# Three graph-attention layers and a gated graph network: first group's attention scores formed on TensorE, layer-norm scale applied in the normalization, new planner durations

## The chip, the cores and the metric

The kernel runs on one core of one Trainium2 chip. Its time is the device time in microseconds of one execution; every figure given as "the time" is the median of several executions. The profile is one execution recorded by the hardware profiler. Each engine of the core (TensorE or PE for matrix products, VectorE or DVE, ScalarE or ACT, GpSimd or POOL, SyncE or SP for transfers) runs its own list of instructions in order; the engines meet at semaphores.

## The reference

There are 128 graphs of 128 nodes with 256 features, all in 32-bit floats. Three attention layers and one recurrent layer follow each other, each on a layer-normalized input and with the input added back:

```python
for l in range(3):                                     # layers 0 to 2
    h  = maximum(layernorm(x), 0)                      # (x - mean) / sqrt(var + eps)
    Wh = h @ W[l]
    e  = (Wh @ a1)[:, :, None] + (Wh @ a2)[:, None, :] # one score for each pair of nodes
    e  = where(e > 0, e, 0.2 * e)
    p  = softmax(where(adj > 0, e, -9e15), axis=-1)
    x  = x + elu(p @ Wh)                               # layer 2: times the node mask first
h = maximum(layernorm(x), 0)
s = h
for i in range(3):                                     # layer 3: gated graph network
    m = A.T @ (s @ weight[i])                          # A = (adj != 0)
    s = gru_cell(m, s)                                 # gates r, z and candidate n
x = x + s
```

## The kernel before, in words

**Tiling.** The 128 graphs are cut into 33 groups (`SIZES`, `FIRST`): the first and the last have two graphs, the others four. A group goes through the three attention layers (`gat`, which calls `attention` once per layer) and then through three recurrent steps (`gru`). In `attention`, node number is the partition and the features lie along the free dimension. In `gru`, features are on the partitions and a group's nodes (512, or 256 in the small groups) are the columns of the products.

**Order.** Nothing is emitted in the order of the source. Every instruction is handed to a planner (`Plan.add`) with its engine, a cost in us, a rank (its due time) and the tiles it reads and writes. `Plan.issue` then runs a list scheduler: on each engine it takes, of the instructions that could start within 0.1 us of the earliest, the one of lowest rank, and moves simulated time on by the cost. Fixed lags stand for semaphores (PE 0.26, DVE and ACT 0.2, POOL 0.15). The order that it finds is the program. So a cost that is changed anywhere can change the order everywhere, though no instruction is added. The costs are small functions: `pe(cols)` at L260, `dve(cols)`, `act(cols)`. The ranks put attention of group 0 at -9, -7 and -5, of group 1 at -6.5, -4.5 and -2.5, and the preparation of the recurrent weights (`SETUP`) at -4; a recurrent step i of group g has rank 3g + i.

**Preparation.** `attention_weights` computes, per layer, the two vectors W·a1 and W·a2 on VectorE (L304, tile `wa`), which stand feature by feature on the partitions; TensorE transposes them and ScalarE copies them (L316) into `va`, where every partition holds both vectors whole. The recurrent weights are products of `gweight` and `w_ih` (L380, tile `wcp`, copied by L387). All of them come before any recurrent step of groups 0 and 1 (`last_setup`).

**Attention, groups 0 and 1** (`far` is false for g < 2). `stats` takes mean and variance (L423, L425), the negative mean `nm` (L430), and on GpSimd variance plus epsilon (L432) and its power of -0.5, `rs` (L434). ScalarE forms `xn` = relu(x - mean) (L507) *without* the scale. A score is one VectorE instruction, `scr` (L515): `xn` times the scalar `rs` of the node times a vector of `va`, summed over the features into `e`; there are two per graph. TensorE turns the second score into a row (L546); VectorE adds the two scores and masks them by a minimum with `cap` (L557, once per graph). Then leaky ReLU (L569), maximum (L571), exponential on ScalarE (L575), reciprocal and product with it (L582 to L586), a transpose on TensorE (L599, `atp`), and a VectorE product of the transposed weights with `rs` (L606, `at`), which puts the scale back. `ahp` (L627) is the product of the attention weights with `xn`, copied to `ah` by ScalarE (L634), `hp` (L646) the product with W; L660 to L664 form elu and the sum in `xo`.

**Attention, groups from 2 on** (`far`). The scale is applied in the normalization: `nm` is multiplied by `rs` (L503) and the activation has `rs` as its scale; the score has the constant 1.0 in place of `rs`. Row and transpose go by way of DRAM (`er`, `at`) instead of TensorE.

**Recurrent steps.** `agp` (L813) aggregates over the graph, copied to `ag` (L821); `nn`, `r`, `z`, `ni` (L790) are the gate products, twelve per half of 128 features; L843 to L880 are the gates on ScalarE and VectorE.

**Buffers.** PSUM has the tags `gat` (2 banks), `gru` (5) and `tr` (1); the pool `gw` has two buffers per tag, `ah` among them.

The cost of the narrow products and the two places where the scale enters before:

```python
    def pe(cols):
        return 0.035 + cols / 600 if cols <= P else 0.01 + cols / 600
...
                scale=rs.t[:, b : b + 1] if far else 1.0,
...
                scr.t, xn.t[:, b, :], 1.0 if far else rs.t[:, b : b + 1], VA[l].t[:, s, :],
...
                rs.t.rearrange("p (g o) -> p g o", o=1).to_broadcast([P, n, N]), op=OP.mult,
```

Of the kernel before, what the change touches and what calls it, by code (L numbers as in the profile page):

```python
# [185 lines left out]
def kernel(  # L186
# [27 lines left out]
    KD = D // P  # L214
    G = 4
    FAR = 2
    SIZES = [2] + [G] * ((B - 4) // G) + [2]
    NG = len(SIZES)
    FIRST = [sum(SIZES[:g]) for g in range(NG)]
# [20 lines left out]
    def const_val(name, shape):  # L240
        return plan.val(const, name, 1, lambda: const.tile([P, *shape], FT, name=name))

    def val(pool, tag, shape, name, bufs=2, dtype=FT, cut=None):

        def make():
            if pool is None and not rw_pool:
                setup.close()
                rw_pool.append(ctx.enter_context(tc.tile_pool(name="rw", bufs=2)))
            p = rw_pool[0] if pool is None else pool
            t = p.tile([P, *shape], dtype, tag=tag, name=name, bufs=bufs)  # L250
            return t if cut is None else t[:, :cut]
        return plan.val(pool, tag, bufs, make)

    def bank(tag, name):
        n = BANKS[tag]
        return plan.val(
            psum, tag, n, lambda: psum.tile([P, T], FT, tag=tag, name=name, bufs=n)
        )

    def pe(cols):  # L260
        return 0.035 + cols / 600 if cols <= P else 0.01 + cols / 600

    def dve(cols):
        return 0.12 + cols / 1000
# [16 lines left out]

    W, VA = [], []

    def attention_weights(l, w, a):
        rank = 1.5 * l - 8.0
        wt, va = const_val(f"w_{l}", [KD, D]), const_val(f"va_{l}", [2, D])
        first = l - 11.2
        load(256, first, lambda: nc.sync.dma_start(  # L290
            wt.t, w.rearrange("(k p) o -> p k o", p=P)), writes=[wt])
        ar = val(su, "ar", [2 * D], f"ar_{l}")
        load(2, first - 0.1, lambda: nc.sync.dma_start(
            ar.t[:1, :], a.rearrange("n o -> o n")), writes=[ar])

        ab = bank("gat", f"ab_{l}")
        add("PE", pe(T), rank, lambda: nc.tensor.matmul(
            ab.t, ones[:1, :], ar.t[:1, :], start=True, stop=True), reads=[ar], writes=[ab])
        wa = val(su, "wa", [2, KD], f"wa_{l}")
        vp = bank("gat", f"vp_{l}")  # L300

        def one(s, k):
            scr = val(su, "scr", [D], f"scr_{l}_{k}_{s}")
            add("DVE", dve(D) + 0.08, rank, lambda: nc.vector.scalar_tensor_tensor(  # L304
                scr.t, wt.t[:, k, :], 1.0, ab.t[:, s * D : (s + 1) * D], op0=OP.mult, op1=OP.mult,
                accum_out=wa.t[:, s, k : k + 1],
            ), reads=[wt, ab], writes=[scr, (wa, (s, k))])
            c = s * KD + k
            add("PE", 0.11, rank, lambda: nc.tensor.transpose(
                vp.t[:, c * P : (c + 1) * P], wa.t[:, s, k : k + 1].to_broadcast([P, P]), ident  # L310
            ), reads=[(wa, (s, k))], writes=[(vp, c)])

        for s in range(2):
            for k in range(KD):
                one(s, k)
        add("ACT", act(T), rank, lambda: nc.scalar.copy(  # L316
            va.t.rearrange("p s d -> p (s d)"), vp.t), reads=[vp], writes=[va])
        W.append(wt)
        VA.append(va)

    for l, (w, a) in enumerate(((w0, a0), (w1, a1), (w2, a2))):
        attention_weights(l, w, a)
# [91 lines left out]
    def stats(xt, n, name, rank, takes):  # L414

        st = val(gw, "st", [G, 6], f"st_{name}", cut=n)
        mv = val(gw, "mv", [G, 2], f"mv_{name}", cut=n)
        nm = val(gw, "nm", [G], f"nm_{name}", cut=n)
        ve = val(gw, "ve", [G], f"ve_{name}", cut=n)
        rs = val(gw, "rs", [G], f"rs_{name}", bufs=3, cut=n)  # L420

        def one(b):
            add("DVE", dve(D), rank, lambda: nc.vector.bn_stats(st.t[:, b, :], xt.t[:, b, :]),  # L423
                reads=[(xt, b)], writes=[(st, b)], takes=[mv, nm, ve, rs, *takes])
            add("DVE", 0.13, rank, lambda: nc.vector.bn_aggr(mv.t[:, b, :], st.t[:, b, :]),  # L425
                reads=[(st, b)], writes=[(mv, b)])

        for b in range(n):
            one(b)
        add("DVE", 0.16, rank, lambda: nc.vector.tensor_scalar(  # L430
            nm.t, mv.t[:, :, 0], -1.0, None, op0=OP.mult), reads=[mv], writes=[nm])
        add("POOL", 0.3, rank, lambda: nc.gpsimd.tensor_scalar(  # L432
            ve.t, mv.t[:, :, 1], EPS, None, op0=OP.add), reads=[mv], writes=[ve])
        add("POOL", 1.04, rank, lambda: nc.gpsimd.tensor_tensor(  # L434
            rs.t, ve.t, mhalf[:, :n], op=OP.pow), reads=[ve], writes=[rs])
        return nm, rs
# [54 lines left out]
    def attention(g, l, xt, cap, xo):  # L491
# [2 lines left out]
        rank = 3.0 * g - lead(g) + 2.0 * l  # L494
        xn = val(gw, "xn", [G, D], f"xn_{name}", cut=n)
        e = val(gw, "e", [2, G], f"e_{name}")
        far = g >= FAR
        nm, rs = stats(xt, n, name, rank, [xn, e, xo, cap])

        if far:
            add("DVE", 0.16, rank, lambda: nc.vector.tensor_mul(nm.t, nm.t, rs.t),  # L503
                reads=[nm, rs], writes=[nm])

        def centred(b):
            add("ACT", 0.45, rank, lambda: nc.scalar.activation(  # L507
                xn.t[:, b, :], xt.t[:, b, :], AF.Relu, bias=nm.t[:, b : b + 1],
                scale=rs.t[:, b : b + 1] if far else 1.0,
            ), reads=[(xt, b), nm, *([rs] if far else [])], writes=[(xn, b)])  # L510


        def score(b, s):
            scr = val(gw, "scr", [D], f"scr_{name}_{b}_{s}")
            add("DVE", dve(D), rank, lambda: nc.vector.scalar_tensor_tensor(  # L515
                scr.t, xn.t[:, b, :], 1.0 if far else rs.t[:, b : b + 1], VA[l].t[:, s, :],
                op0=OP.mult, op1=OP.mult, accum_out=e.t[:, s, b : b + 1],
            ), reads=[(xn, b), rs, VA[l]], writes=[scr, (e, (s, b))])

        for b in range(n):  # L520
            centred(b)
        for b in range(n):
            score(b, 1)
            score(b, 0)

# [3 lines left out]


        em = val(gw, "em", [G, N], f"em_{name}", cut=n)
        if far:
            de = plan.val(
                dram, f"de{n}", 2, lambda: dram.tile([P, n], FT, tag=f"de{n}", name=f"de_{name}")
            )
            er = val(gw, "er", [N * G], f"er_{name}")
            load(2, rank, lambda: nc.sync.dma_start(de.t, e.t[:, 1, :n]),
                reads=[(e, (1, b)) for b in range(n)], writes=[de], takes=[er, em])
            load(64 * n, rank, lambda: nc.sync.dma_start(
                er.t[:, : N * n], de.t.rearrange("p n -> (p n)").partition_broadcast(P)  # L540
            ), more=1.6, reads=[de], writes=[er])
        else:
            e2 = bank("gat", f"e2_{name}")
# [15 lines left out]
                cap.t[:, b, :], op0=OP.add, op1=OP.min,  # L559
            ), reads=[er if far else (e2, b), (e, (0, b)), cap], writes=[(em, b)])  # L560

        for b in range(0 if far else n):
            row(b)
        for b in range(n):
            masked(b)
        nmx = val(gw, "nmx", [G], f"nmx_{name}", cut=n)
        sm = val(gw, "sm", [G], f"sm_{name}", cut=n)
        ri = val(gw, "ri", [G], f"ri_{name}", cut=n)
# [3 lines left out]
            nmx.t, em.t, axis=AX.X, op=OP.max, negate=True), reads=[em], writes=[nmx])  # L572

        def power(b):
            add("ACT", 0.42, rank, lambda: nc.scalar.activation(  # L575
                em.t[:, b, :], em.t[:, b, :], AF.Exp, bias=nmx.t[:, b : b + 1],
                accum_out=sm.t[:, b : b + 1],
            ), reads=[(em, b), nmx], writes=[(em, b), (sm, b)])
# [4 lines left out]
        if l == 2:  # L583
            add("DVE", 0.16, rank, lambda: nc.vector.tensor_mul(
                ri.t, ri.t, nmT.t[:, FIRST[g] : FIRST[g] + n]), reads=[ri, nmT], writes=[ri])
        add("DVE", dve(n * P), rank, lambda: nc.vector.tensor_tensor(  # L586
            em.t, em.t, ri.t.rearrange("p (g o) -> p g o", o=1).to_broadcast([P, n, N]), op=OP.mult
        ), reads=[em, ri], writes=[em])

# [13 lines left out]
        if not far:  # L603
            for b in range(n):
                turn(b)
            add("DVE", dve(n * P), rank, lambda: nc.vector.tensor_tensor(  # L606
                at.t, atp.t[:, : n * P].rearrange("p (g i) -> p g i", g=n),
                rs.t.rearrange("p (g o) -> p g o", o=1).to_broadcast([P, n, N]), op=OP.mult,
            ), reads=[atp, rs], writes=[at])

        def turned_weights(b):
            if far:
# [57 lines left out]
    def gat(g):  # L670
# [27 lines left out]
            reads=[nm, rs], writes=[nm])  # L698

        def normed(b):  # L700
            add("ACT", 0.45, rank, lambda: nc.scalar.activation(
                hn.t[:, b, :], xt.t[:, b, :], AF.Relu, bias=nm.t[:, b : b + 1],
                scale=rs.t[:, b : b + 1],
            ), reads=[(xt, b), nm, rs], writes=[(hn, b)])
# [264 lines left out]
```

## Time and profile before

| what | value |
|---|---|
| median of 3 executions | 2757.75 us (2756.5 to 2758.16) |
| the profiled execution | 2757.73 us, span 2756.0 us |
| TensorE busy | 2712.8 us, 98% of the span |
| VectorE busy | 2082.3 us, 76% |
| ScalarE busy | 1280.4 us, 46% |
| GpSimd busy | 293.7 us, 11% |
| matrix instructions | 9563 |

The span runs from the first to the last instruction; the execution's own time is 1.7 us longer. "Busy" is the union of an engine's recorded instructions. In the profile's name for a group of instructions, `out<-in` gives the tiles, `x` the count, and the number behind the engine the source line. A 32-bit product is recorded as two matrix instructions (passes), so a product of 128 columns counts as x2. Transposes are single instructions. "Idle before, releaser" is the time for which the engine waited just before the group, and what ended the wait.

### The profile page before, as it was taken

Reading aid. Unit: us, or ns where it says so; the run is one execution under the profiler, and the core shown is the slowest. Engines: PE = TensorE matmul, PEld = TensorE weight load, DVE = VectorE, ACT = ScalarE, POOL = GpSimd, SP = SyncE. Lnnn points to the kernel's source line nnn. Section 1 sums busy time; section 2 is a strip of 40 time slices with the busy share of each in tenths; the row PEclk is TensorE's granted clock in tenths of the full one; section 3 lists DMA queues with packets and bytes.
Section 4 is the critical chain, followed back from the end, with each engine's and each line's share of the span. In section 5 each row is a group of like instructions: output and inputs, shape, how many; then the busy total and the mean of one; then the engine's idle time right before and its main releaser. Section 6 shows DMA issues by size and latency. Waiting matters only on the chain.

```text
span 2756.0 us, 32248 instructions
## 1 busy us (share of the span) xinstructions
PE 2712.8 (98%) x9563; PEld 1569.7 (57%) x9563; DVE 2082.3 (76%) x5541; ACT 1280.4 (46%) x2709; POOL 293.7 (11%) x369
## 2 busy tenths in 40 slices
PE   7899999999999999999999999999999999999998
PEld 4755555555555555555555555555555555555546
DVE  7778888778768887877788687778768886876643
ACT  4545444444444454444454445444444444444433
POOL 1111110101101101110111111111101010100000
PEclk9999999999999999999999999999999999999999
DMA  3113334433324433333333344323334333333310
GB/s 91 51 58 100 88 95 101 111 94 86 97 80 108 108 99 78 101 91 96 105 97 83 87 105 104 109 75 91 97 88 110 103 93 86 94 74 93 79 44 12
DMA packets 503094, 245.30 MB, mean 89 GB/s; under 512 B 280580, under 2 KB 472068, under 8 KB 502919
## 3 DMA queue, kind: packets, MB, share of 16 engines
q1 hardware_dynamic: 502918, 243.25, 33.5%
q8 instruction: 76, 1.25, 0.2%
q14 instruction: 100, 0.81, 0.1%
HBM read 139.28 MB, written 103.87 MB: 88 GB/s over the span
## 4 chain that ended last, share of the span: by engine, by line
PE 88%; DVE 8%; ACT 2%; DMA 1%; issue 1%; POOL 0%; SPq 0%; DVEq 0%; ACTq 0%; POOLq 0%
PE z L790 21%; PE r L790 21%; PE hp L646 11%; PE ni L790 11%; PE nn L790 10%; PE ahp L627 6%; PE agp L813 5%; DVE em L557 1%; DVE scr L515 1%; DVE xo L662 1%; DVE xo L664 1%; DVE d L877 1%; ACT em L575 1%; DVE h L880 1%; DVE n L856 0%
## 5 line engine op out<-in xcount | busy, mean ns | idle before, releaser
L790 PE MATMUL nn<-h,whh 128*128 128x512 f32 (+1 forms) x792 | 395.6, 581 | 1.9 <-DVE h L880 1.9
L790 PE MATMUL r<-ag,wc 128*128 128x512 f32 (+1 forms) x792 | 395.2, 581 | 1.3 <-ACT ag L821 1.3
L790 PE MATMUL ni<-ag,wc 128*128 128x512 f32 (+1 forms) x792 | 394.4, 579 | 1.4 <-ACT ag L821 1.4
L790 PE MATMUL z<-ag,wc 128*128 128x512 f32 (+1 forms) x792 | 394.2, 579 | 0.0
L790 PE MATMUL z<-h,whh 128*128 128x512 f32 (+1 forms) x792 | 394.2, 579 | 0.0
L790 PE MATMUL r<-h,whh 128*128 128x512 f32 (+1 forms) x792 | 394.2, 579 | 0.0
L851 DVE SCALAR_TENSOR_TENSOR n<-r,wn 128x512 f32<-128x512 f32 (+1 forms) x198 | 132.6, 670 | 336.5 <-ACT r L848 336.0
L646 PE MATMUL hp<-w,ah 128*128 128x256 f32 x1536 | 373.2, 381 | 0.5 <-ACT ah L634 0.2
L646 PEld LDWEIGHTS hp<-w,ah 128*128 128x128 f32 x1536 | 290.1, 190 | 131.4 <-issue 95.7
L515 DVE SCALAR_TENSOR_TENSOR scr<-xn,va 128x256 f32<-128x256 f32 x732 | 266.4, 423 | 33.9 <-ACT xn L507 33.6
L848 ACT ACTIVATE r<-r,brz 128x512 f32<-128x512 f32 (+1 forms) x198 | 133.2, 673 | 284.3 <-PE r L790 282.0
L813 PEld LDWEIGHTS agp<-am,hn 128*128 128x128 f32 x1536 | 202.3, 191 | 85.7 <-issue 73.5
L790 PEld LDWEIGHTS ni<-ag,wc 128*128 128x128 f32 x792 | 149.8, 190 | 177.9 <-issue 171.0
L790 PEld LDWEIGHTS r<-h,whh 128*128 128x128 f32 x792 | 149.3, 190 | 169.4 <-issue 162.8
L790 PEld LDWEIGHTS z<-h,whh 128*128 128x128 f32 x792 | 148.7, 190 | 168.3 <-issue 158.3
L821 ACT COPY ag<-agp 128x512 f32<-128x512 f32 (+1 forms) x198 | 113.0, 571 | 263.2 <-PE agp L813 262.8
L790 PEld LDWEIGHTS z<-ag,wc 128*128 128x128 f32 x792 | 148.4, 190 | 142.4 <-issue 138.2
L575 ACT ACTIVATE em<-em,nmx 128x128 f32<-128x128 f32 x384 | 149.4, 391 | 168.2 <-DVE nmx L571 166.4
L790 PEld LDWEIGHTS r<-ag,wc 128*128 128x128 f32 x792 | 146.1, 190 | 135.4 <-issue 120.5
L627 PEld LDWEIGHTS ahp<-at,xn 128*128 128x128 f32 x1536 | 191.3, 195 | 49.4 <-issue 37.6
L813 PE MATMUL agp<-am,hn 128*128 128x128 f32 x1536 | 205.3, 275 | 6.4 <-ACT hn L802 3.9
L526 POOL TENSOR_SCALAR xo<-xo 128x1024 f32<-128x1024 f32 (+1 forms) x66 | 73.2, 1110 | 1215.6 <-DVE xo L664 989.8
(94 smaller groups left out, 3474.1 us busy)
## 6 DMA issues: line engine op xcount, KB each, us to landing
d_hn<-tr_hn SPq DMA_DIRECT2D x116, 256.0 KB, 2.4
hn<-d_hn SPq DMA_DIRECT2D x464, 64.0 KB, 2.3
er<-de SPq DMA_DIRECT2D x90, 256.0 KB, 3.9
d_at<-tr_at SPq DMA_DIRECT2D x90, 256.0 KB, 2.0
at<-d_at SPq DMA_DIRECT2D x360, 64.0 KB, 2.0
x<-in_x_dram SPq DMA_DIRECT2D x31, 512.0 KB, 4.4
d_h<-tr_h SPq DMA_DIRECT2D x31, 512.0 KB, 2.9
h<-d_h SPq DMA_DIRECT2D x124, 128.0 KB, 3.1
```

The costliest lines, as they stand in the source:

```text
L515: add("DVE", dve(D), rank, lambda: nc.vector.scalar_tensor_tensor(scr.t, xn.t[:, b, :], 1.0 if far else rs.t[:, b : b + 1], VA[l].t[:, s, ...
L526: add("POOL", 0.14 + n * D / 1070, rank, lambda: nc.gpsimd.tensor_scalar(xo.t, xt.t, 1.0, -1.0, op0=OP.mult, op1=OP.add), reads=[xt], writ ...
L557: add("DVE", dve(P) + (0.15 if far else 0.05), rank, lambda: nc.vector.scalar_tensor_tensor(em.t[:, b, :], e2_row(b), e.t[:, 0, b : b + 1] ...
L575: add("ACT", 0.42, rank, lambda: nc.scalar.activation(em.t[:, b, :], em.t[:, b, :], AF.Exp, bias=nmx.t[:, b : b + 1], accum_out=sm.t[:, b ...
L627: add("PE", pe(P), rank, lambda: nc.tensor.matmul(summed(ps, b), xn.t[:, b, k * P : (k + 1) * P], turned_weights(b), start=True, stop=True ...
L646: add("PE", pe(D), rank, lambda: nc.tensor.matmul(hp.t[:, b * D : (b + 1) * D], ah.t[:, k, c * P : (c + 1) * P], W[l].t[:, k, :], start=(k ...
L662: add("DVE", dve(T), rank, lambda: nc.vector.scalar_tensor_tensor(u(), hp.t, 0.0, u(), op0=OP.max, op1=OP.add), reads=[hp, *parts], writes ...
L790: nc.tensor.matmul(o, w.t[:, k, c * P : (c + 1) * P], m, start=start, stop=stop)
L813: nc.tensor.matmul(ps.t[:, b * P : (b + 1) * P], s, am.t[:, b, :], start=True, stop=True)
L821: add("ACT", act(TG), quick, lambda: nc.scalar.copy(t.t[:, :TG], ps.t[:, :TG]), reads=[ps], writes=[t])
L848: add("ACT", act(TG) + 0.1, quick, lambda: nc.scalar.activation(r.t[:, :TG], pr.t[:, :TG], AF.Tanh, bias=brz.t[:, cr : cr + 1], scale=0.5) ...
L851: add("DVE", dve(TG), quick, lambda: nc.vector.scalar_tensor_tensor(n.t[:, :TG], r.t[:, :TG], 1.0, wn.t[:, :TG], op0=OP.add, op1=OP.mult), ...
```

## The change

1. **Scale in the normalization, all groups.** The `far` condition at `nm * rs`, at the activation's scale and at the score's scalar goes; groups 0 and 1 now do what the later groups did. The VectorE product with `rs` after the transpose becomes a plain ScalarE copy.
2. **Scores of group 0 on TensorE** (`early`, g < 1). In place of the scores and rows, TensorE transposes `xn` (`xTp`, two banks of tag `gat`), ScalarE copies it to `xT` (a buffer of tag `ah`), and per graph four products of 128 columns accumulate both scores of every pair of nodes in the bank `es` (tag `gru`). One VectorE minimum of `es` with `cap` masks both graphs. `wa` becomes a constant tile, since these products read it.
3. **Planner costs.** `pe` of up to 128 columns loses 0.026 us; `bn_aggr` 0.13 to 0.08; normalizations 0.45 to 0.55; exponential 0.42 to 0.55; score +0.03; product with the reciprocal +0.1.

```diff
     FAR = 2
+    EARLY = 1
...
-        return 0.035 + cols / 600 if cols <= P else 0.01 + cols / 600
+        return 0.009 + cols / 600 if cols <= P else 0.01 + cols / 600
...
-        wa = val(su, "wa", [2, KD], f"wa_{l}")
+        wa = const_val(f"wa_{l}", [2, KD])
...
-            add("DVE", 0.13, rank, lambda: nc.vector.bn_aggr(mv.t[:, b, :], st.t[:, b, :]),
+            add("DVE", 0.08, rank, lambda: nc.vector.bn_aggr(mv.t[:, b, :], st.t[:, b, :]),
...
-        if far:
-            add("DVE", 0.16, rank, lambda: nc.vector.tensor_mul(nm.t, nm.t, rs.t),
-                reads=[nm, rs], writes=[nm])
+        add("DVE", 0.16, rank, lambda: nc.vector.tensor_mul(nm.t, nm.t, rs.t),
+            reads=[nm, rs], writes=[nm])
 
         def centred(b):
-            add("ACT", 0.45, rank, lambda: nc.scalar.activation(
+            add("ACT", 0.55, rank, lambda: nc.scalar.activation(
                 xn.t[:, b, :], xt.t[:, b, :], AF.Relu, bias=nm.t[:, b : b + 1],
-                scale=rs.t[:, b : b + 1] if far else 1.0,
-            ), reads=[(xt, b), nm, *([rs] if far else [])], writes=[(xn, b)])
+                scale=rs.t[:, b : b + 1],
+            ), reads=[(xt, b), nm, rs], writes=[(xn, b)])
...
-            add("DVE", dve(D), rank, lambda: nc.vector.scalar_tensor_tensor(
-                scr.t, xn.t[:, b, :], 1.0 if far else rs.t[:, b : b + 1], VA[l].t[:, s, :],
+            add("DVE", dve(D) + 0.03, rank, lambda: nc.vector.scalar_tensor_tensor(
+                scr.t, xn.t[:, b, :], 1.0, VA[l].t[:, s, :],
                 op0=OP.mult, op1=OP.mult, accum_out=e.t[:, s, b : b + 1],
-            ), reads=[(xn, b), rs, VA[l]], writes=[scr, (e, (s, b))])
+            ), reads=[(xn, b), VA[l]], writes=[scr, (e, (s, b))])
...
-        if far:
+        if early:
+
+            xT = val(gw, "ah", [KD, T], f"xT_{name}")
+            es = bank("gru", f"es_{name}")
+
+            def features(k):
+                ps = bank("gat", f"xTp_{name}_{k}")
+
+                def turn(b):
+                    add("PE", 0.11, rank, lambda: nc.tensor.transpose(
+                        ps.t[:, b * P : (b + 1) * P], xn.t[:, b, k * P : (k + 1) * P], ident
+                    ), reads=[(xn, b)], writes=[(ps, b)], takes=[xT])
+
+                for b in range(n):
+                    turn(b)
+                add("ACT", act(n * P), rank, lambda: nc.scalar.copy(
+                    xT.t[:, k, : n * P], ps.t[:, : n * P]), reads=[ps], writes=[(xT, k)])
+
+            def pairs(b):
+                def fn():
+                    o = es.t[:, b * P : (b + 1) * P]
+                    for k in range(KD):
+                        v = xT.t[:, k, b * P : (b + 1) * P]
+                        e1, e2 = (WA[l].t[:, s, k : k + 1].to_broadcast([P, P]) for s in range(2))
+                        nc.tensor.matmul(o, e2, v, start=(k == 0), stop=False)
+                        nc.tensor.matmul(o, v, e1, start=False, stop=(k == KD - 1))
+
+                add("PE", 4 * pe(P), rank, fn,
+                    reads=[xT, WA[l]], writes=[(es, b)], takes=[em])
+
+            for k in range(KD):
+                features(k)
+            for b in range(n):
+                pairs(b)
+        elif far:
...
+        if early:
+            add("DVE", dve(n * P), rank, lambda: nc.vector.tensor_tensor(
+                em.t, es.t[:, : n * P].rearrange("p (b i) -> p b i", b=n), cap.t, op=OP.min
+            ), reads=[es, cap], writes=[em])
...
-            add("ACT", 0.42, rank, lambda: nc.scalar.activation(
+            add("ACT", 0.55, rank, lambda: nc.scalar.activation(
                 em.t[:, b, :], em.t[:, b, :], AF.Exp, bias=nmx.t[:, b : b + 1],
...
-        add("DVE", dve(n * P), rank, lambda: nc.vector.tensor_tensor(
+        add("DVE", dve(n * P) + 0.1, rank, lambda: nc.vector.tensor_tensor(
             em.t, em.t, ri.t.rearrange("p (g o) -> p g o", o=1).to_broadcast([P, n, N]), op=OP.mult
...
-            add("DVE", dve(n * P), rank, lambda: nc.vector.tensor_tensor(
-                at.t, atp.t[:, : n * P].rearrange("p (g i) -> p g i", g=n),
-                rs.t.rearrange("p (g o) -> p g o", o=1).to_broadcast([P, n, N]), op=OP.mult,
-            ), reads=[atp, rs], writes=[at])
+            add("ACT", act(n * P), rank, lambda: nc.scalar.copy(
+                at.t.rearrange("p b i -> p (b i)"), atp.t[:, : n * P]), reads=[atp], writes=[at])
...
-            add("ACT", 0.45, rank, lambda: nc.scalar.activation(
+            add("ACT", 0.55, rank, lambda: nc.scalar.activation(
                 hn.t[:, b, :], xt.t[:, b, :], AF.Relu, bias=nm.t[:, b : b + 1],
```

## The prediction

> **What bounds the kernel now.** I read the page first: TensorE is busy for 98% of the span, and the chain that ended last is TensorE for 88%.
>
> ```profile
> span 2756.0 us, 32248 instructions
> PE 2712.8 (98%) x9563; PEld 1569.7 (57%) x9563; DVE 2082.3 (76%) x5541; ACT 1280.4 (46%) x2709; POOL 293.7 (11%) x369
> PE   7899999999999999999999999999999999999998
> PE 88%; DVE 8%; ACT 2%; DMA 1%; issue 1%; POOL 0%; SPq 0%; DVEq 0%; ACTq 0%; POOLq 0%
> ```
>
> So time is TensorE's work plus its 43.2 us of idle time. Next I cut the span into stretches (columns: stretch, length, busy us and instructions of PE, PEld, DVE, ACT, POOL, then TensorE's granted clock).
>
> ```profile
> 0.00:50.00 50.00, 41.78 (x178) 27.54 (x179) 32.67 (x124) 23.91 (x63) 8.99 (x19) 1.00 0.41 120
> 50.00:80.00 30.00, 18.04 (x73) 13.94 (x72) 22.77 (x86) 12.90 (x35) 6.08 (x8) 0.72 0.06 17
> 80.00:100.00 20.00, 15.48 (x80) 13.47 (x79) 18.32 (x57) 8.55 (x25) 2.59 (x3) 0.91 0.13 29
> 100.00:300.00 200.00, 195.73 (x752) 122.03 (x752) 157.07 (x443) 100.84 (x230) 23.42 (x30) 1.00 0.30 83
> 300.00:2600.00 2300.00, 2296.18 (x7971) 1306.62 (x7970) 1788.44 (x4708) 1081.32 (x2260) 249.74 (x304) 1.00 0.36 94
> 2600.00:2756.00 156.00, 145.57 (x517) 86.10 (x515) 63.05 (x125) 52.87 (x99) 2.89 (x5) 0.99 0.13 35
> ```
>
> Idle is 8.2, 12.0, 4.5, 4.3, 3.8 and 10.4 us. From 300 to 2600 us nothing can be won (3.8 of 2300). What the change touches lies in the first 100 us, where 24.7 us are idle; some 8 of them pass before there is anything to do. The timeline of TensorE shows the rest, and a second loss:
>
> ```profile
> 42.87 1.05 PE L627 MATMUL ahp<-at,xn 128*128 128x128 f32 x8
> 53.02 0.32 PE L546 MATMUL e<-ident,e 128*128 128x128 f32 x1 [0.87 <-DVE em L557]
> 56.57 0.66 PE L599 MATMUL atp<-ident,em 128*128 128x128 f32 x2 [3.22 <-DVE em L586]
> 57.75 2.08 PE L627 MATMUL ahp<-at,xn 128*128 128x128 f32 x8 [0.52 <-DVE at L606]
> 70.25 1.09 PE L599 MATMUL atp<-ident,em 128*128 128x128 f32 x4 [6.79 <-DVE nm L697]
> 72.13 3.75 PE L627 MATMUL ahp<-at,xn 128*128 128x128 f32 x16 [0.29 <-DVE at L606]
> 79.67 0.61 PE L813 MATMUL agp<-am,hn 128*128 128x128 f32 x4
> 95.17 0.63 PE L599 MATMUL atp<-ident,em 128*128 128x128 f32 x4 [3.63 <-DVE em L586]
> ```
>
> After an idle stretch the same products take twice as long: eight passes of L627 take 1.05 us at 42.87 and 2.08 at 57.75. Against warm rows the slow ones between 57 and 80 us cost 4.6 us (1.0 at 57.75, 1.0 at 60.28, 0.5, 1.8 and 0.3 from 70.25), and one at 96.68 costs 1.5. The first recurrent product comes at 79.67 us; from there work is plentiful but for one stop at 91. The question is when that product comes. VectorE's timeline shows why it is late:
>
> ```profile
> 31.13 0.81 DVE L515 SCALAR_TENSOR_TENSOR scr<-xn,rs,va 128x256 f32<-128x256 f32 x1
> 34.61 0.17 DVE L582 RECIPROCAL ri<-sm 128x4 f32<-128x4 f32 x1
> 43.70 0.69 DVE L662 SCALAR_TENSOR_TENSOR xo<-hp,xo 128x512 f32<-128x512 f32 x1 [6.09 <-ACT t L660]
> 50.63 0.48 DVE L515 SCALAR_TENSOR_TENSOR scr<-xn,rs,va 128x256 f32<-128x256 f32 x1
> ```
>
> Group 1's reciprocal (34.61) was ready at 32.9, when ScalarE ended the exponentials, but stood behind group 0's scores; then VectorE is idle for 6.1 us while TensorE is full; then VectorE is full from 48 to 70 while TensorE is idle.
>
> **What the Trainium skill says.** "TensorE: Matmul & The Clock Gate", Part 1 (the HAM clock gate): TensorE drops to half rate after an idle window of about 3.4 us and needs as long a busy one to recover. The trace agrees (3.22 us of idle, then 2.08 for 1.05). "VectorE: DVE Perf Modes", the TRN2 errata section: a fixed cost per VectorE instruction, so few wide ones are cheaper than many narrow ones; here two L557 of 128 columns take 0.61 us together, and L606, which reads PSUM as the new minimum will, takes 0.42 for 256. "Perfetto Trace Analysis", Optimization Strategy: where the most contended engine changes over time, look for gaps within each regime; that is the reading above.
>
> **The change, part by part.**
>
> *VectorE, group 0.* Start-to-start, a score takes 0.41 us (50.63 to 51.04). Per layer four go (1.63), two L557 (0.61) become one minimum (0.42), the product L606 (0.42) moves to ScalarE, and the product of `nm` and `rs` comes (0.16). Net -2.1, three layers -6.2 us. *Group 1.* With the constant in place of `rs` a score takes 0.35 (at 73.25 and after): eight save 0.5; L606 (0.69) goes; +0.16. Net -1.0, three layers -3.0 us.
>
> *TensorE.* Sixteen warm passes of L627 take 1.78 us (111.72 to 113.50), so a product takes 0.22. Per layer eight products (1.78), four transposes at 0.11 and two rows less: +2.0, three layers +6.0 us; layer 0 runs at the slow clock and takes about 2 more where TensorE waits anyway. That a stationary or moving operand is one column repeated is not shown as a product; its bounds are 0.22 each (as any other) and twice that, so 0 to +5 more; I take 0.22. What hides the 6 us is the preparation, L380: between 32 and 52 us TensorE fills its time with it, and what is pushed out can run in the holes of 53 to 70 us, which it also keeps warm. Without that cover the whole 6.0 is paid.
>
> *ScalarE.* Per layer two copies of 256 (0.37 each) for `xT`, one `at` copy (0.37 and 0.58), and 0.09 more for each of 18 normalizations (0.59 against 0.50): 6.7 us in all. ScalarE is busy 36.8 of the first 80 us: hidden.
>
> *The added wait.* The normalization now waits for GpSimd's `rs` and a VectorE product. In layer 1 `rs` ends at 30.42; `nm` follows at 30.8, both `xn` by 31.9, transposes and copies by 33.1, products by 35.4, the minimum by 35.8, against 33.78 for the masks now: +2.0 on group 0's path. Behind the waiting normalization on ScalarE stand weight copies (L387) and group 1's exponentials, at most 1 us. In layer 1 most is absorbed: group 0's L627 at 38 to 40 us was already waiting for TensorE (group 1's products and L380 between), so `xo` moves from 43.7 to about 44.5. In layer 2 the scores waited from 47.7 to 50.6 behind group 1's `xo`, and the masks ended at 53.7; the new route needs `rs` 47.2, `xn` 48.6, copies 49.9, minimum 52.7, all +0.8: no loss.
>
> *Group 1.* Its reciprocal comes 1.7 us earlier, its transposed weights no longer queue on VectorE, so its `hp` and `xo` (47.97 to 50.6) move some 3 us into VectorE's hole. Layer 1 then starts earlier, and VectorE has 3.3 us less in 50 to 63 (three scores 2.06 with one slowed to 1.25, a mask 0.35, L606 0.37, half a us in group 1's scores); its own later `xn` costs 0.85, covered by `cap` work. So TensorE's continuous stretch starts at about 66 instead of 70.25, the slow clock loses some 2 us less, and the first recurrent product comes near 73.5 instead of 79.67: **-6 us**. The bound on that gain: work before 79.67 is 79.67 - 20.2 idle = 59.5; plus 6.0, minus up to 4 of slow clock, plus 7 at the very start gives 68.5, so at most -11. Next is late whatever comes second: group 1's layer 2.
>
> *The stop at 91 us.* VectorE is busy 9.8 of 10 us there. L606 and shorter scores take 1.2 off; the later `xn` adds up to 0.85. I take **-1**, between -3 and +1.
>
> *Planner durations.* No work is added; the order everywhere can shift. From 100 to 2600 us there are 8.1 us of idle, the tail has 10.4; below nothing the gain ends near -3. A loss isn't shown by this trace; 0.3 us in each of 28 groups would be +8. I take 0.
>
> Sum against the profiled execution: 2757.73 - 6 - 1 = **2750.7**; span 2749. The profiled execution is within 0.02 of the median, so it stands for both.
>
> **Rivals.** *(1) No gain, 2757 (2754 to 2761):* group 0's longer path (+2 a layer, +6 unabsorbed) cancels VectorE's relief, or the planner puts the products late. For it: VectorE was idle at 37.6 to 43.7, so relief before that may be worth nothing. Against: it was full from 48 to 70. *(2) Slower, 2763.8:* TensorE becomes the bound in the start. It is busy 21.7 of 22 us from 30 to 52; if the preparation pushed out by the new products is still unfinished when group 0's state is ready, the first recurrent product waits for all 6.0 us. It decides from the point where L380 ends after about 72 us. For it: preparation ends at 52 now, so 20 us of slack stand against it. *(3) The new durations put small stops into the later groups:* +8.4 on the forecast, 2759; speaks for it that the exponential is set to 0.55 while its start-to-start time is 0.4, against it that TensorE has a full queue there.
>
> **How the numbers follow.** Forecast 0.55 (2744 to 2754, of which 0.45 below 2752.2), rival 1 0.22, rival 2 0.13, rival 3 0.10 (half of it slower). A measurement can tell about 0.2%, 5.5 us, from no change. Faster 0.45, same 0.10 + 0.22 + 0.05 = 0.37, slower 0.13 + 0.05 = 0.18. The range goes from -11 -3 and a little (2743) to 2761, the end of rival 1, with rival 2 and part of the largest gains left out. Cases of both signs count, so: the likeliest alone is 2744 to 2754.
>
> **What would show it.** L813 first at 72 to 75 us; TensorE idle of 52 to 70 us at half of 11.4; L380 products after 53 us; no L515 of group 0; group 1's first `xo` before 47 us; 300 to 2600 us under 5 us idle. I am wrong if L813 comes after 78, or if it comes early and the time does not follow, which would put the loss into later groups.

## The result and the profile after

The changed kernel takes 2764.63 us (median of 10, 2762.92 to 2766.6), the kernel before 2758.14 (2756.5 to 2759.86): ratio 1.0023, 95% interval 1.0014 to 1.0033. It is slower by 6.5 us; 2750.7 was forecast, so the miss is 13.9 us. The profiled execution took 2762.92 us, its span is 2761.1 us.

The page of the changed kernel, its first lines:

```profile
span 2761.1 us, 32374 instructions
PE 2720.1 (99%) x9617; PEld 1579.7 (57%) x9617; DVE 2072.3 (75%) x5514; ACT 1286.6 (47%) x2721; POOL 288.0 (10%) x369
```

TensorE is busy 7.3 us longer and idle 41.0 us instead of 43.2. By stretches (columns as in the prediction; the last two, behind the clock, are the share of time in which the DMA engines are busy, and GB/s), changed kernel:

```profile
0.00:100.00 100.00, 83.58 (x389) 63.83 (x390) 64.20 (x241) 50.84 (x134) 17.60 (x30) 0.93 0.25 71
100.00:180.00 80.00, 80.00 (x347) 56.67 (x347) 56.12 (x162) 41.60 (x97) 9.53 (x12) 1.00 0.20 60
180.00:300.00 120.00, 110.61 (x374) 63.62 (x373) 92.79 (x262) 54.78 (x121) 14.03 (x18) 0.97 0.32 80
300.00:600.00 300.00, 295.05 (x1029) 167.72 (x1028) 235.39 (x626) 140.15 (x296) 33.79 (x39) 1.00 0.35 96
600.00:2600.00 2000.00, 1999.26 (x6947) 1138.35 (x6947) 1558.07 (x4092) 943.34 (x1972) 208.93 (x263) 1.00 0.36 95
```

The same cuts of the kernel before:

```profile
0.00:100.00 100.00, 75.29 (x328) 54.95 (x329) 73.75 (x267) 45.37 (x121) 17.65 (x30) 0.90 0.25 71
180.00:300.00 120.00, 116.56 (x406) 65.53 (x405) 98.58 (x267) 59.51 (x134) 12.38 (x16) 1.00 0.36 97
300.00:600.00 300.00, 299.07 (x1052) 172.16 (x1051) 237.70 (x629) 140.44 (x291) 32.11 (x41) 1.00 0.35 93
```

The start did fill: 16.4 us of idle time in the first 100 us instead of 24.7. But from 180 to 600 us idle time grew from 3.4 + 0.9 to 9.4 + 4.9 us, in a part of the kernel where no instruction was changed. TensorE's timeline of the changed kernel, at the rows that answer to those shown of before:

```profile
36.52 0.39 PE L557 MATMUL es<-wa,xT 128*128 128x128 f32 x2
38.51 3.62 PE L682 MATMUL hp<-w,ah 128*128 128x256 f32 x16
46.10 1.89 PE L682 MATMUL hp<-w,ah 128*128 128x256 f32 x8
76.40 1.23 PE L849 MATMUL agp<-am,hn 128*128 128x128 f32 x4 [1.18 <-ACT h L756]
94.35 0.67 PE L826 MATMUL nn<-h,whh 128*128 128x256 f32 x2 [3.30 <-ACT em L613]
96.29 1.06 PE L637 MATMUL atp<-ident,em 128*128 128x128 f32 x4
222.74 3.75 PE L663 MATMUL ahp<-at,xn 128*128 128x128 f32 x16 [5.49 <-DVE scr L515]
```

The first recurrent product comes at 76.40 us, not 79.67: 3.3 us earlier. At 222.74 TensorE has stood for 5.5 us and comes back at the slow clock (3.75 us where 1.95 is usual). SyncE's list (SPq is its queue of transfers) shows one reason (columns: start, duration, operation):

```profile
213.00 0.34 SPq L460 DMA_DIRECT2D d_at<-tr_at  x1
216.52 0.40 SPq L713 DMA_DIRECT2D x<-in_x_dram  x1
217.03 1.86 SPq L464 DMA_DIRECT2D at<-d_at  x4
```

The load of `x` for group 6 waits for its buffer until 216.52, and the four transfers that TensorE needs are queued behind it. (The profile puts the end of TensorE's wait down to VectorE; the transfers, issued from 217.03 us on, took 4.2 us to land, which is when the wait ends.) Between 180 and 600 us this stop and seven waits for `ag`, ScalarE's copy of the aggregate, make up 10.2 of 14.3 us of idle time (columns: what waited for what, us in total, times, longest):

```profile
PE ahp L663 <- DVE scr L515: 5.5, 1, 5.5
PE agp L849 <- ACT ag L857: 2.7, 4, 0.7
PE ni L826 <- ACT ag L857: 2.0, 3, 0.7
```

The kernel before has two waits for `ag` there (at 257.80 and 343.96 us, 0.68 us each) and no stop longer than 1.1 us.

### The profile page after: what moved, and what is told of

Its sections match the earlier page's. It is cut to its first block, busy times and chain, and to the rows that moved or that the text cites. A ratio compares the mean times of both kernels' runs of the same rounds, so it can differ in the third digit from the quotient of the medians.

```text
span 2761.1 us, 32374 instructions
## 1 busy us (share of the span) xinstructions
PE 2720.1 (99%) x9617; PEld 1579.7 (57%) x9617; DVE 2072.3 (75%) x5514; ACT 1286.6 (47%) x2721; POOL 288.0 (10%) x369
## 4 chain that ended last, share of the span: by engine, by line
PE 94%; DVE 3%; ACT 1%; DMA 1%; issue 1%; SPq 0%; POOL 0%; ACTq 0%; DVEq 0%; POOLq 0%
PE r L826 23%; PE z L826 23%; PE ni L826 11%; PE hp L682 11%; PE nn L826 11%; PE ahp L663 6%; PE agp L849 6%; PE wcp L382 1%; DVE xo L698 0%; DVE xo L700 0%; DVE scr L515 0%; DMA d_hn<-tr_hn 0%; DVE d L913 0%; DMA hn<-d_hn 0%; DVE st L425 0%
## 5 line engine op out<-in xcount | busy, mean ns | idle before, releaser
L682 PE MATMUL hp<-w,ah 128*128 128x256 f32 x1536 | 359.7, 380 | 0.7 <-ACT ah L670 0.7
L515 DVE SCALAR_TENSOR_TENSOR scr<-xn,va 128x256 f32<-128x256 f32 x756 | 278.5, 424 | 32.1 <-ACT xn L507 31.8
L670 ACT COPY ah<-ahp 128x512 f32<-128x512 f32 (+1 forms) x198 | 112.1, 572 | 223.1 <-PE ahp L663 221.6
```

Source lines behind the costliest of these rows:

```text
L515: add("DVE", dve(D) + 0.03, rank, lambda: nc.vector.scalar_tensor_tensor(scr.t, xn.t[:, b, :], 1.0, VA[l].t[:, s, :], op0=OP.mult, op1=OP. ...
L670: add("ACT", act(n * P), rank, lambda: nc.scalar.copy(ah.t[:, k, : n * P], ps.t[:, : n * P]), reads=[ps], writes=[(ah, k)])
L682: add("PE", pe(D), rank, lambda: nc.tensor.matmul(hp.t[:, b * D : (b + 1) * D], ah.t[:, k, c * P : (c + 1) * P], W[l].t[:, k, :], start=(k ...
```

## The experiments

I held three theories. A: the planner's new order for the later groups costs what the start had won, and more. B: the products of group 0 are to blame. C: the order is a lottery with no system. All medians stand beside 2758 to 2759 us for the kernel before on the same chip; the numbers in brackets are the ratio to it and its 95% interval.

**Taking the parts apart.** First the changed kernel with the old durations (parts 1 and 2):

```diff
-        return 0.009 + cols / 600 if cols <= P else 0.01 + cols / 600
+        return 0.035 + cols / 600 if cols <= P else 0.01 + cols / 600
...
-            add("ACT", 0.55, rank, lambda: nc.scalar.activation(
+            add("ACT", 0.42, rank, lambda: nc.scalar.activation(
                 em.t[:, b, :], em.t[:, b, :], AF.Exp, bias=nmx.t[:, b : b + 1],
```

(and the other durations likewise).

> The changed kernel with the planner's old durations: parts 1 and 2 of the change alone. Theory A (the new durations set an order that starves TensorE between 180 and 600 us): the stop of 5.5 us near 217 us is gone, the 3 us won at the start are kept, time 2749 to 2756, below the kernel before. Theory B (the products of group 0 are to blame: 6 us of added work, and recurrent steps that start earlier run into the attention of the next groups): a stop of several us stays near 200 to 240 us, time 2761 to 2766 as in the changed kernel. Theory C (the order is a lottery, any edit moves it by some us): no system, anything from 2752 to 2768.

Measured 2770.23 (1.0044, 1.0031 to 1.0056): slower than either kernel, outside the ranges of A, B and C. Next, the kernel before with the new durations alone, the same edit the other way round:

> The kernel before with the new durations and nothing else: part 3 alone. No work is added. Theory A: slower than before, 2761 to 2768, with stops between 180 and 600 us. Theory B: 2756 to 2760, as before. Theory C: anything from 2752 to 2768.

Measured 2794.4 (1.0124, 1.0108 to 1.0139). No instruction differs from the kernel before, and it takes 36 us more: the direction as in A, but far outside its range and C's. Then the changed kernel without products:

```diff
-    EARLY = 1
+    EARLY = 0
```

> The changed kernel without the products of group 0 (EARLY = 0): parts 1 and 3. Theory A: 2761 to 2768, stops after 180 us as in the changed kernel. Theory B: 2755 to 2759, the stop is gone with the products. Theory C: anything from 2752 to 2768.

Measured 2801.12 (1.0156, 1.0142 to 1.0169), again outside all three ranges. Last, that with the old durations too:

> The changed kernel without the products and with the old durations: part 1 alone, the scale in the normalization. Theories A and B both: 2754 to 2759, about as before, since VectorE has 3 us less work in group 1 and its normalization waits 0.9 us longer in each layer. Theory C: anything from 2752 to 2768, which would show that even this small edit moves the later order.

Measured 2764.81 (1.0022, 1.0013 to 1.0032), against 2754 to 2759 expected of A and B; only C's wide range holds it. The parts do not add up: the durations cost 36 us both without part 1 (2758 to 2794) and with it (2765 to 2801), but with the products they gain 5.6 (2770.2 to 2764.6). The trace of the run without products, new durations, shows where most of its 43 us went. TensorE's longest waits from 600 to 2600 us, and one place of its timeline:

```profile
PE agp L849 <- ACT ag L857: 16.2, 24, 0.7
PE ni L826 <- ACT ag L857: 8.1, 12, 0.7
```

```profile
1147.35 0.38 PE L849 MATMUL agp<-am,hn 128*128 128x128 f32 x2
1148.41 1.16 PE L849 MATMUL agp<-am,hn 128*128 128x128 f32 x8 [0.68 <-ACT ag L857]
1150.24 1.16 PE L849 MATMUL agp<-am,hn 128*128 128x128 f32 x8 [0.68 <-ACT ag L857]
```

Once in every second group the aggregation of the second half (`agp`) stands on TensorE's list straight behind that of the first, and in the two kernels near 2800 us the first stands behind one of the next group. All use the one bank `tr`, so TensorE waits until ScalarE has copied it out (0.59 us and the signals), twice here, and once more where a later product (`ni`) needs the copy. These 36 waits have 24.3 us of idle time. From start to start each costs more: at 1147.35 two passes that otherwise take 0.22 us take 1.06, so by my estimate 0.84 us each and some 30 us together. From 180 to 600 us this run is idle for 16.2 us, where the kernel before is for 4.4.

The lists of instructions show how this comes about. In the kernel before none of the 99 recurrent steps has this place; in the changed kernel 2 have it, with old durations 5 (in either count one of them has two products in between), and in the two runs near 2800 us 13 and 14, from group 6 or 4 on in the last step of every second group. Also, the order repeats: the list of the kernel before repeats itself every three groups from group 4 on, that of the changed kernel every three from group 7 on, those of the two kernels near 2800 us every two. With old durations TensorE's list is the same as before from group 8 on, with or without products. So the planner settles into one of a few repeating orders, and in these runs what it planned for the first groups decided which. The changed kernel settles into a good one (0.7 us idle from 600 to 2600 us); what it loses, it loses between 180 and 600 us, on the way there.

**Testing that count.** One of the new durations set back, the cost of the product with the reciprocal:

```diff
-        add("DVE", dve(n * P) + 0.1, rank, lambda: nc.vector.tensor_tensor(
+        add("DVE", dve(n * P), rank, lambda: nc.vector.tensor_tensor(
             em.t, em.t, ri.t.rearrange("p (g o) -> p g o", o=1).to_broadcast([P, n, N]), op=OP.mult
```

> The changed kernel with one of its seven durations set back: the product with the reciprocal costs the planner dve(512) as before, not 0.1 more. No instruction changes. In the order that comes out, 13 of 99 recurrent steps have the second half's aggregation straight behind the first half's, on the one bank that both use, as in the two runs that took 2794 and 2801 (13 and 14 such places; 2 in the changed kernel, none in the kernel before). Theory A (those places are the loss): 2785 to 2805. If the loss of those runs came from the durations being wrong as such, or from scores left on VectorE: 2762 to 2767.

Measured 2791.12 (1.0117, 1.0102 to 1.0133), as A expected. And another one, the exponential at 0.42:

> The changed kernel with another single duration set back: the exponential costs the planner 0.42, not 0.55. No instruction changes. In the order that comes out 2 of 99 recurrent steps have the second aggregation straight behind the first, as in the changed kernel. Theory A: 2758 to 2768. If any duration set back costs as much as the one that gave 2791: over 2780.

Measured 2759.09 (1.0004, 0.9996 to 1.0012), within A. With the changed kernel's own instructions, the time goes from 2759 to 2791 by planner costs alone, and the count tells which side it falls on. It does not tell the 2759 from the changed kernel's 2764.6: both have 2 such places.

**The stop at 217 us.** The changed kernel, with one entry of SyncE's list moved after planning:

```diff
+        late, behind = self.moved
+        order.remove(late)
+        order.insert(order.index(behind) + 1, late)
         for op in order:
```

> The changed kernel with one entry of SyncE's list moved: the load of x for group 6 is issued after the four transfers that bring back group 3's second attention weights, not in front of them. If that load caused the stop of 5.5 us near 217 us (SyncE waited 3.1 us for its buffer, and the four transfers then landed in 4.2 us, 1.8 elsewhere): the stop falls to 1 to 3 us, TensorE stays at full clock behind it, time 2757 to 2761. If the stop is only TensorE having run ahead of attention: stop of 4 us or more, time 2763 to 2766.

Measured 2766.61 (1.0026, 1.0016 to 1.0036): no gain on 2764.63, though 2757 to 2761 was expected if the load was the cause. TensorE's timeline of this run (of its fastest execution, 2761.8 us):

```profile
215.56 2.02 PE L670 MATMUL ahp<-at,xn 128*128 128x128 f32 x16 [1.21 <-DMA at<-d_at]
220.00 1.78 PE L858 MATMUL agp<-am,hn 128*128 128x128 f32 x6 [2.42 <-ACT hn L746]
221.95 6.57 PE L689 MATMUL hp<-w,ah 128*128 128x256 f32 x16 [0.16 <-ACT ah L677]
```

The load did cause most of that stop: it fell from 5.49 to 1.21 us. The time did not follow. Group 2's recurrent state is late as well (2.42 us), and 16 passes of `hp` now run slow (6.57 us against 3.62). Taking one wait away uncovers the next: from the `hp` ahead of the stop to the first `nn` behind it the changed kernel takes 24.6 us (210.20 to 234.75), this run 24.9 (207.30 to 232.20).

**Keeping the order.** To see the instructions without the planner, the order of the kernel before was computed first, and the new kernel emitted in it; what is new stands at the place of what it replaces.

```diff
+    model = build(0, False).issue()
+    plan = build(EARLY, True)
+    order = plan.follow(model)
...
-        plan.issue()
+        plan.emit(order)
```

> Part 1 alone (the scale in the normalization), emitted in the order of the kernel before; TensorE's, SyncE's and GpSimd's lists are the same as before. Theory A: 2754 to 2760, so that the 2765 of the run with part 1 alone was the order. If part 1 itself costs by its later normalization, 2763 to 2766 again.

Measured 2764.76 (1.0022, 1.0014 to 1.0029): as the second expectation said, part 1 costs 5.5 us when the start isn't planned anew. The first recurrent product comes at 83.81 us, 4.1 later, and TensorE is idle for 14.4 us between 50 and 80 us instead of 12.0. I take it that the normalization's longer path does this where the list offers no other work.

> Parts 1 and 2 of the change, emitted in the order of the kernel before: every instruction that both have keeps its place, the new ones stand where the scores stood. From group 0's last layer on TensorE's list is the same as before. Theory A (the order that the planner finds for the later groups is what costs): 2752 to 2760, the start's effect alone. Theory B (the products' 6 us of TensorE work are paid in full): 2762 to 2767. A new theory D (both are true in part: old durations with products gave 2770, without them 2765, though TensorE's lists are the same from group 0's last layer on): 2761 to 2764.

Measured 2772.87 (1.0056, 1.0043 to 1.0068), outside all three. The first recurrent product comes at 96.19 us, 16.5 later than before: the products, put where the scores stood, hold up the preparation behind them on TensorE's list. This start is a bad one of my making and says nothing on the planner's; in it a start 16.5 us late, the products' own work included, comes out 13.6 us late at the end.

**Exchanging start and rest.** The decisive runs take the order of one plan up to group 1's first recurrent product and that of another from there on.

```diff
+    before = build(0, False, False).issue()
+    start = build(EARLY, FOLD, True).issue()
+    plan = build(EARLY, FOLD, True)
+    order = plan.follow(before, start)
```

> Part 1's instructions (no products). Up to group 1's first recurrent product the order is the one that the new durations give, from there on the order of the kernel before. With the new durations alone, without this change of the rest, the same instructions took 2801; their first recurrent product came at 74.4 us and group 1's at 128.5, against 79.7 and 134.4 before. Theory A (the later order is what cost; an earlier start carries through one for one when the later order is good): 2751 to 2756, faster than before. If the early start can't be kept because attention of groups 2 and 3 is not further on: 2757 to 2763, with stops between 180 and 300 us.

Measured 2754.58 (0.9988, 0.9980 to 0.9996): inside A's range, and faster than both kernels. A's reason for it, that an early start carries through one for one, is not what the trace shows. TensorE is 4.4 us ahead of the kernel before at the aggregation of 118.49 us (before: 122.92), then, where the two orders meet (the joint), it stands for want of group 0's state and runs on at the slow clock:

```profile
118.49 1.16 PE L920 MATMUL agp<-am,hn 128*128 128x128 f32 x8 [0.85 <-ACT hn L909]
122.12 0.70 PE L897 MATMUL nn<-h,whh 128*128 128x256 f32 x2 [2.04 <-DVE h L987]
124.19 1.06 PE L897 MATMUL z<-h,whh 128*128 128x256 f32 x2
```

At group 1's first gate product it is 0.6 us ahead (133.87, before 134.42). The range was met in part by luck.

> Part 1's instructions again, the other way round: up to group 1's first recurrent product the order that the old durations give (2765 with the old order throughout), from there on the order that the new durations give. Theory A: the loss sits in the later order, so 2790 to 2803, with the stops of 0.7 us in every second group. If the loss came from the start, 2762 to 2768.

Measured 2805.55 (1.0175, 1.0161 to 1.0189): A's direction, 2.5 us over its range. The same instructions thus take 2755 or 2801 behind the start of the new durations, and 2765 or 2806 behind that of the old ones: the rest is worth 41 to 47 us, the start 4 to 10 (the old durations' rest is that of before from group 8 on, not sooner).

> The changed kernel's instructions, its own order up to group 1's first recurrent product, and the order of the kernel before from there on. The first recurrent product came at 76.4 us in the changed kernel, group 1's at 131.3. Theory A: 2753 to 2758, some 2 to 3 us more than the same without products, since the products delay the start by 2 us and add 6 us of work. If the early start can't be kept: 2759 to 2764.

Measured 2757.52 (0.9997, 0.9989 to 1.0006), within A's range. These are the changed kernel's instructions and its start; only the later order is that of before, and it takes 7.1 us less, more than the 6.5 that were lost. It does so although the same stop at the joint takes it from 2.0 us ahead of the kernel before (aggregation at 120.97) to 1.9 behind: group 1's first gate product comes at 136.36 us, in the changed kernel at 131.28. TensorE's idle time from 180 to 600 us falls to 4.7 us:

```profile
180.00:300.00 120.00, 116.60 (x407) 65.76 (x406) 99.42 (x270) 60.97 (x136) 12.65 (x17) 1.00 0.35 94
300.00:600.00 300.00, 298.72 (x1047) 171.54 (x1046) 235.53 (x624) 139.61 (x289) 32.11 (x41) 1.00 0.35 94
```

For the measured loss theory A stands: the later order costs it. C holds in so far as small edits choose among a few orders. B is right on a smaller point: without the products the same construction is 2.9 us faster.

## Why the prediction was wrong

*The step that failed: "Planner durations ... I take 0".* The 6.5 us are the later order: with the order of before in its place they are gone. Of the miss of 13.9 us this is 7.1 (2764.6 against 2757.5). The other 6.8 are the gain of 7 that I had put on the start and the stop at 91: with the order of before behind it the change comes out 0.7 us below the kernel before, which is within the noise (some 4 us of it are lost at the joint, as told above). I saw the risk as rival 3, gave it 0.10 and priced it at 0.3 us a group, at most +8; the runs show +36 for the same durations on the kernel before, and some 7 in the changed kernel. "No work is added" was true and said nothing, and "TensorE has a full queue there" was wrong: it is full only as long as the list offers other work at each wait.

*"-6" for the first recurrent product: mis-sized, and not worth its size at the end.* It moved by 3.3 us. Group 1's `hp` did move ahead (38.51, before 44.45; its `xo` from 47.97 to 42.36, 5.6 us instead of 3), but in front of group 0's, whose `hp` came at 46.10 and `xo` at 48.70, 5.0 us later where I had 0.8 (first line: before; the others: the changed kernel):

```profile
44.45 3.72 PE L646 MATMUL hp<-w,ah 128*128 128x256 f32 x16
42.36 1.29 DVE L698 SCALAR_TENSOR_TENSOR xo<-hp,xo 128x512 f32<-128x512 f32 x2 [2.28 <-ACT t L696]
48.70 0.69 DVE L698 SCALAR_TENSOR_TENSOR xo<-hp,xo 128x512 f32<-128x512 f32 x1 [0.63 <-ACT t L696]
```

I assumed that what sets the start would keep its place while the rest moved up.

*Products: "0.22 each", right; hidden, wrong.* Group 0's layer 1 products took 1.78 us as worked out (34.96 to 36.74), the minimum came at 36.94 for 35.8. In these products a repeated column costs no more than any other operand. But the products do not help the start. VectorE's timeline of the changed kernel, in the cover that I had named:

```profile
31.08 0.16 DVE L503 TENSOR_TENSOR nm<-nm,rs 128x2 f32<-128x2 f32 x1 [0.62 <-POOL rs L436]
36.94 0.42 DVE L601 TENSOR_TENSOR em<-es,cap 128x256 f32<-128x256 f32 x1 [5.70 <-PE es L557]
```

VectorE was relieved where it then stood idle for 5.7 us, as rival 1's argument had it. With the new durations the first recurrent product comes at 74.37 us without products and at 76.40 with them; with the old ones at 76.17 and 77.60. TensorE's list of that last pair is the same from group 0's last layer on, and the products cost 5.4 us there (2764.8 to 2770.2), most of the 6.0 that rival 2 charged. That is a difference of medians alone: the executions without products spread from 2759.9 to 2769.0, and the two that were profiled took 2768.8 and 2768.3, so their traces do not show it. In the exchanged runs the products cost 2.9.

*The start's gain was given back.* Against the kernel before, in us of TensorE's idle time: -8.3 up to 100 us, -0.8 up to 180, +10.0 from 180 to 600, -2.2 from 600 to 2600, -0.9 behind it; in sum -2.2, and +7.3 of busy time (the products' 6.0, and the slow clock) gives the +5.1 of the two spans. The signs I named came true in part: the first `agp` came at 76.4, between the 72 to 75 of the forecast and the 78 of failure; idle time of 52 to 70 us fell from 11.4 to 4.2; preparation went on past 53 us; "it comes early and the time does not follow, which would put the loss into later groups" is what happened.

*The stop at 91 us: the size about right, by luck.* It is 3.30 us and ends at 94.35; before 3.63 and 0.89 behind it. But what ends it is a gate product that now stands first on the list. The transposes for which TensorE waited before come at 96.29, 1.1 us later than the 95.17 of before, though the scores ahead of them are shorter.

*Rival 2's 2763.8* is near the measured time for another reason: the preparation was not late (its last product starts before 54 us), so its point of decision was never reached.

What stays open: why the durations lead to the bad repeating order without products and to a good one with them. The lists show that they do, not which place in the start decides it. No run took such a place out of a list by hand, so the price of one is read from its waits. And the later order of before was put behind a planned start in the two exchanged runs only, where the joint itself brings a stop of 2.04 us; what parts 1 and 2 are worth in a good order throughout is not shown.

## What to carry to other kernels

Where a planner writes the order, its costs are part of the program: a change of durations, or of a few instructions early on, can change the order of everything behind it, and has to be priced as a change of the whole list. Before timing, compare the lists, and count the places where an instruction stands straight behind the one whose buffer it needs. That count finds a bad repeating order; it did not find the 7 us that the changed kernel loses before it settles into a good one. To price an edit itself, hold the order and exchange start and rest; an early gain counts only if the work that follows is also ready earlier.

## What the runs showed of the hardware

A wait of 0.68 us for a single bank costs little once, but three of them in every two groups made up 24 us of idle time (16.2 + 8.1 from 600 to 2600 us, new durations without products). And in the run with the moved load two short stops within 6 us (1.21 and 2.42) were followed by 16 passes at 0.41 us where 0.23 is usual, with a granted clock of 0.66 from 220 to 230 us. The Trainium skill, "TensorE: Matmul & The Clock Gate", Part 1, speaks of an idle window of about 3.4 us; here no single stop was that long, and the clock fell all the same. It still stood at 1.00 from 210 to 220 us, so it fell only behind the second stop. The 3.22 us of the kernel before, where the prediction says that the trace agrees, were short of 3.4 too. And in the first exchanged run a stop of 2.04 us that ended at 122.12 us was followed by gate products of 1.06 us instead of 0.59. How much idle time is enough is not shown. The run with the moved load by stretches:

```profile
210.00:220.00 10.00, 6.37 (x29) 3.84 (x27) 8.76 (x28) 5.78 (x11) 1.26 (x2) 1.00 0.33 107
220.00:230.00 10.00, 9.15 (x29) 7.06 (x30) 5.01 (x17) 4.05 (x8) 0.00 (x0) 0.66 0.59 170
```
